# Interleaving layer 0's mixing of one pair with layer 1 of another, and subtracting tanh results before they are weighed

## The chip, the cores and the metric

The kernel runs on one core of a Trainium2 chip. The metric is device time in microseconds (us) of one execution; the numbers below are medians of the runs of a kernel, and lower is better. Every comparison uses runs on the same chip, in rounds in which the kernel before and the other kernel take turns.

The engines are named as the profile names them: PE is TensorE's matmul, PEld its weight loads, DVE is VectorE, ACT ScalarE, POOL GpSimd, SP SyncE. L156 is line 156 of the kernel in question.

## The reference, cut to what matters

Four graph layers run one after another on `x` (8 batches, 2048 nodes, 64 features), each followed by a residual addition and a layer norm over the features. The change concerns the end of layer 0 and all of layer 1:

```python
# layer 0, its end ("mixing")
def attn_scores(f):
    return jnp.tanh(f @ fcW + fcb) @ av
pair = jnp.stack([industry, g], axis=2)
coefs2 = jax.nn.softmax(attn_scores(pair), axis=-1)
out = jnp.einsum('bnk,bnkf->bnf', coefs2, pair)
x = _layernorm(x + out)
# layer 1
A_td = A + jnp.eye(n); dinv = rsqrt(A_td.sum(1)); A_hat = dinv[:, None] * A_td * dinv[None, :]
x = _layernorm(x + jnp.einsum('bnd,kd->bnk', jnp.einsum('bmd,nm->bnd', x, A_hat), W))
# layers 2 and 3: not touched
```

A softmax over two scores is a sigmoid of their difference. So the weights need only `(tanh(f0) - tanh(f1)) @ av`, and whether the subtraction happens before or after the product with `av` is free to choose. A batch pair of layer 1 needs all of that pair's layer 0, but nothing of another pair's.

## The kernel before

The eight batches are four *pairs*; two batches' 64 features sit side by side in 128 columns. The 2048 nodes are four *chunks* of 512. So mixing is 16 chunks, one after another, and then layer 1 takes the four pairs.

```python
def layernorm(pool, r, dst, groups=2 * JT):          # r: 128 x 512, 8 groups of 64
    mean = ...; nc.vector.tensor_reduce(mean, r, AX.X, ALU.add)
    xc = pool.tile([P, groups, F], F32, tag="ln_c", name="ln_c", bufs=1)
    nc.vector.scalar_tensor_tensor(xc, mean..., -1.0 / F, r, op0=ALU.mult, op1=ALU.add)
    nc.scalar.activation(r, xc, AF.Square)
    var = ...;  nc.vector.tensor_reduce(var, r, AX.X, ALU.add)
    vare = ...; nc.vector.tensor_scalar(vare, var, 1.0 / F, EPS, op0=ALU.mult, op1=ALU.add)
    rstd = ...; nc.gpsimd.tensor_tensor(rstd, vare, neg_half[:, :groups], ALU.pow)   # L155
    nc.vector.tensor_tensor(dst, xc, rstd..., ALU.mult)                              # L156

def mm(*args, **kw):                                 # pinned: keeps its place in the stream
    tc.keep_in_program_order(nc.tensor.matmul(*args, **kw))
# ... cut ...
for p in range(NP):                                  # mixing
    for c in range(NCH):
        # four indirect gathers (GpSimd) -> gn;  ut <- u0_hbm
        pg = to_rows(...)                            # four transposes
        nc.scalar.activation(gt, pg, AF.Identity, bias=-1.0)
        nc.tensor.matmul(pi, lhsT=bd_ind, rhs=ut, start=True, stop=True)
        nc.vector.tensor_copy(ind, pi)               # the "ind copy"
        tt = []
        for b in range(2):
            for k, src in enumerate((ind, gt)):
                nc.tensor.matmul(pf, lhsT=fcz[:, b, :], rhs=src, start=True, stop=True)
                nc.scalar.activation(t1, pf, AF.Tanh, bias=fcb_col)
                tt.append((b, k, t1))
        for i, (b, k, t1) in enumerate(tt):          # four weighing products
            nc.tensor.matmul(pd, lhsT=avz[:, b, k, :], rhs=t1, start=i == 0, stop=i == 3)
        nc.scalar.activation(th, pd, AF.Tanh, scale=0.5)
        # three DVE instructions: ind <- gt + (th + 1)/2 * (ind - gt)
        pt = to_rows(...)                            # back: four transposes
        nc.vector.tensor_tensor(r, pt..., r, ALU.add)   # r was loaded with x
        layernorm(mp, grouped(r), grouped(xn[...]))
for p in range(NP):                                  # layer 1
    nc.vector.tensor_tensor(y, xn[:, p], dinv..., ALU.mult)
    u = product(..., plus_identity=True)             # split y in halves, 128 + 32 matmuls
    for c in range(NCH):
        evacuate(ut, u[c]); po = ...                 # four output products
        nc.vector.tensor_tensor(r, po, dinv..., ALU.mult)
        nc.gpsimd.tensor_tensor(r, r, xs, ALU.add)
        layernorm(lp, grouped(r), grouped(xs))
```

An instruction that is pinned with `keep_in_program_order` keeps its place among the pinned instructions of its engine. All others are placed by the scheduler when the kernel is built. Either way an engine's order is then fixed: it does not change at run time. Note that `layernorm` goes from DVE to ACT, back to DVE, to GpSimd for the power, and back to DVE.

Of the kernel before, what the change touches and what calls it, by code (L numbers as in the profile page):

```python
# [30 lines left out]
F32 = mybir.dt.float32  # L31
# [25 lines left out]
def tile_gnn_fast(  # L57
# [144 lines left out]
    hs_hbm = dram.tile([N, BF + 8], F32, name="hs_hbm")  # L202
    gs_hbm = dram.tile([N, BF], F32, name="gs_hbm")
# [427 lines left out]

    hy_scope.close()
    const2 = ctx.enter_context(tc.tile_pool(name="const2", bufs=1))
    xn = const2.tile([P, NP, NT, P], F32, name="xn")
    with tc.tile_pool(name="mix", bufs=1) as mp, tc.tile_pool(name="mix_ps", bufs=1, space=PSUM) as mps:
        bd_ind = on_diagonal(mp, w_ind, "bd_ind")
        fcb_col = column(mp, fc_b, "fcb_col", 1)
        av_col = column(mp, av, "av_col", 1)

        fcz = mp.tile([P, 2, P], F32, name="fcz")  # L640
        nc.vector.memset(fcz, 0.0)

        avz = mp.tile([P, 2, 2, P], F32, name="avz")
        nc.vector.memset(avz, 0.0)
        for b in range(2):
            s = slice(b * F, (b + 1) * F)
            nc.sync.dma_start(fcz[s, b, :], fc_w)
            nc.vector.tensor_copy(avz[:, b, 0, s], av_col.to_broadcast([P, F]))
            nc.vector.tensor_scalar(avz[:, b, 1, s], avz[:, b, 0, s], -1.0, None, op0=ALU.mult)
        g_rows = gs_hbm[:].rearrange("n (p f) -> (n p) f", f=P)  # L650
        for p in range(NP):
            for c in range(NCH):
                gn = mp.tile([P, JT, P], F32, tag="gn", name="gn", bufs=2)
                for j in range(JT):
                    nc.gpsimd.indirect_dma_start(  # L655
                        out=gn[:, j, :], out_offset=None, in_=g_rows,
                        in_offset=bass.IndirectOffsetOnAxis(ap=rank4[:, p, c * JT + j:c * JT + j + 1], axis=0),
                    )
                ut = mp.tile([P, C], F32, tag="ut", name="ut", bufs=3)
                nc.sync.dma_start(ut, u0_hbm[p][:, cols(c)])  # L660
                pg = to_rows(mps, "tr", 2, [gn[:, j, :] for j in range(JT)])
                gt = mp.tile([P, C], F32, tag="gt", name="gt", bufs=2)
                nc.scalar.activation(gt, pg, AF.Identity, bias=-1.0)
                pi = mps.tile([P, C], F32, tag="mm", name="pi", bufs=6)
                nc.tensor.matmul(pi, lhsT=bd_ind, rhs=ut, start=True, stop=True)
                ind = mp.tile([P, C], F32, tag="ind", name="ind", bufs=2)
                nc.vector.tensor_copy(ind, pi)

                tt = []
                for b in range(2):  # L670
                    for k, src in enumerate((ind, gt)):
                        pf = mps.tile([P, C], F32, tag="mm", name="pf", bufs=6)
                        nc.tensor.matmul(pf, lhsT=fcz[:, b, :], rhs=src, start=True, stop=True)
                        t1 = mp.tile([P, C], F32, tag="t1", name="t1", bufs=4)
                        nc.scalar.activation(t1, pf, AF.Tanh, bias=fcb_col)
                        tt.append((b, k, t1))
                pd = mps.tile([P, C], F32, tag="mm", name="pd", bufs=6)
                for i, (b, k, t1) in enumerate(tt):
                    nc.tensor.matmul(pd, lhsT=avz[:, b, k, :], rhs=t1, start=i == 0, stop=i == 3)
                th = mp.tile([P, C], F32, tag="th", name="th", bufs=1)  # L680
                nc.scalar.activation(th, pd, AF.Tanh, scale=0.5)
                nc.vector.tensor_tensor(ind, ind, gt, ALU.subtract)
                nc.vector.scalar_tensor_tensor(ind, th, 1.0, ind, op0=ALU.add, op1=ALU.mult)
                nc.vector.scalar_tensor_tensor(ind, ind, 0.5, gt, op0=ALU.mult, op1=ALU.add)
                pt = to_rows(mps, "tr", 2, [ind[:, cols(j, P)] for j in range(JT)])
                r = mp.tile([P, JT, P], F32, tag="r", name="r", bufs=3)
                load_x(r, p, c)
                nc.vector.tensor_tensor(r, pt.rearrange("p (t f) -> p t f", f=P), r, ALU.add)
                layernorm(mp, grouped(r), grouped(xn[:, p, c * JT:(c + 1) * JT, :]))


    with tc.tile_pool(name="l1", bufs=1) as lp, tc.tile_pool(name="l1_ps", bufs=1, space=PSUM) as lps:
        bd_w1 = on_diagonal(lp, w1_t, "bd_w1")
        for p in range(NP):
            y = lp.tile([P, NT, P], F32, tag="y", name=f"y{p}", bufs=2)
            nc.vector.tensor_tensor(
                y, xn[:, p, :, :], dinv[:, :, None].to_broadcast([P, NT, P]), ALU.mult
            )
            u = product(lp, lps, lambda k, y=y: y[:, k * JT:(k + 1) * JT, :], plus_identity=True)
            for c in range(NCH):  # L700
                ut = lp.tile([P, C], F32, tag="ut", name="ut", bufs=3)
                evacuate(ut, u[c])
                po = lps.tile([P, JT, P], F32, tag="mm", name="po", bufs=4)
                for j in range(JT):
                    nc.tensor.matmul(po[:, j, :], lhsT=ut[:, cols(j, P)], rhs=bd_w1, start=True, stop=True)
                r = lp.tile([P, JT, P], F32, tag="r", name="r", bufs=2)
                ts = slice(c * JT, (c + 1) * JT)
                xs = xn[:, p, ts, :]
                nc.vector.tensor_tensor(
                    r, po, dinv[:, ts, None].to_broadcast([P, JT, P]), ALU.mult  # L710
                )
                nc.gpsimd.tensor_tensor(r, r, xs, ALU.add)
                layernorm(lp, grouped(r), grouped(xs))
# [6 lines left out]
    with tc.tile_pool(name="l2c", bufs=1) as cp:  # L720
# [3 lines left out]
        with tc.tile_pool(name="apt", bufs=1) as ap_:  # L724
# [31 lines left out]
            with tc.tile_pool(name="apt1", bufs=1) as a1, tc.tile_pool(  # L756
                name="apt_ps", bufs=1, space=PSUM
            ) as aps:
                for c in range(NCH):
                    u = [aps.tile([P, C], F32, tag=f"u{p}", name=f"u{p}") for p in range(NP)]  # L760
                    acc = a1.tile([P, C], F32, tag="acc", name="acc", bufs=2)
                    for t in range(NT):
# [9 lines left out]
                        for p in range(NP):  # L772
                            nc.tensor.matmul(  # L773
                                u[p], lhsT=xn[:, p, t, :], rhs=pt, start=t == 0, stop=t == NT - 1
                            )
# [12 lines left out]
        with tc.tile_pool(name="l2", bufs=1) as lp, tc.tile_pool(name="l2_ps", bufs=1, space=PSUM) as lps:  # L788
# [7 lines left out]
            for p in range(NP):  # L796
                u1n = lp.tile([P, NT, P], F32, tag="u1n", name=f"u1n{p}")
                u = product(lp, lps, lambda k, p=p: xn[:, p, k * JT:(k + 1) * JT, :])
# [47 lines left out]
    with tc.tile_pool(name="l3", bufs=1) as lp, tc.tile_pool(name="l3_ps", bufs=1, space=PSUM) as lps:  # L846
# [21 lines left out]
        nc.tensor.matmul(pm, lhsT=bd_v, rhs=b2c, start=True, stop=True)  # L868
        nc.vector.tensor_tensor(b1s, pm, b1, ALU.add)

        pending = []

        def later(n, f):

            pending.append([n, f])

        def tick():
            for e in pending:
                e[0] -= 1
            while pending and pending[0][0] <= 0:  # L880
                pending.pop(0)[1]()

# [829 lines left out]
```

## Time and profile before

2304.5 us, median of four runs (2302.7 to 2307.0). The profiled execution took 2301.2 us.

The lines of its profile are in the prediction: what the engines do in five windows of this kernel. Read them for the stage in which PE stands idle although another stage has plenty of independent PE work. Layers 2 and 3, from 742.6 us to the end, took 1558.6 us; the change doesn't concern them. In a line of the waits the order is: engine, what waits, `<-` the engine and tile that released it, the total in us, how often, the longest. A line of the timeline is start, duration, engine, line, operation, and in brackets how long the engine had been idle and what ended that.

### The profile page before, as it was taken

How to read it: one execution, taken by the hardware profiler on the slowest of the kernel's cores; microseconds unless marked ns; L12 is line 12 of the kernel's file. 1: busy time of each engine (PE TensorE's matmuls, PEld its weight loads, DVE VectorE, ACT ScalarE, POOL GpSimd, SP SyncE). 2: the span in 40 equal slices, each digit the busy share in tenths (PEclk: the TensorE clock that was granted, in tenths of full speed). 3: DMA queues.
4: the chain of work that ended last, by engine and by line, in shares of the span. 5: the costliest groups of instructions: out<-in, count | busy, mean ns of one | idle time of the engine just before them, and what ended most of it. 6: DMA issues, size and time to landing. Idle time of an engine off the chain costs nothing.

```text
span 2301.2 us, 19853 instructions
## 1 busy us (share of the span) xinstructions
PE 2009.9 (87%) x7382; PEld 1293.3 (56%) x7382; DVE 1119.7 (49%) x1895; ACT 361.7 (16%) x610; POOL 468.2 (20%) x432
## 2 busy tenths in 40 slices
PE   5379977887993999979999999999996999899994
PEld 3258863335882444447447446546543777777873
DVE  4347983554544122222882784685585334341322
ACT  2412323331111111101001001000000011111110
POOL 0155524550332332310010010011001001020202
PEclk8779998999995999989999999999998999999997
DMA  7712223220000000010000000000000223210000
GB/s 245 233 38 63 84 95 91 69 60 1 1 1 12 0 19 19 19 41 1 9 8 3 7 7 5 5 10 5 5 7 11 73 70 82 72 30 1 19 1 20
DMA packets 92586, 88.64 MB, mean 39 GB/s; under 512 B 62976, under 2 KB 63232, under 8 KB 92416
## 3 DMA queue, kind: packets, MB, share of 16 engines
q1 hardware_dynamic: 65072, 61.35, 9.3%
q10 hardware_dynamic: 23568, 16.95, 2.5%
q0 software_dynamic: 3840, 8.98, 1.5%
q8 instruction: 60, 0.98, 0.2%
q14 instruction: 46, 0.38, 0.1%
HBM read 66.22 MB, written 21.04 MB: 38 GB/s over the span
## 4 chain that ended last, share of the span: by engine, by line
PE 47%; DMA 8%; DVE 7%; POOL 3%; issue 2%; ACT 1%; SPq 0%; DVEq 0%; ACTq 0%; POOLq 0%
PE py L826 17%; PE u L773 10%; PE u L459 9%; PE u L171 8%; DMA a<-in_adj_t 7%; DVE a L932 2%; POOL ln_r L155 1%; PE pr L171 1%; PE tr L137 1%; DVE xg L115 1%; POOL r L838 1%; DVE ln_c L145 1%; DVE ln_v L151 1%; ACT r L149 0%; PE s L764 0%
## 5 line engine op out<-in xcount | busy, mean ns | idle before, releaser
L826 PE MATMUL py<-wp,xg 128*128 128x512 f32 x1024 | 448.6, 597 | 8.4 <-DVE pr L831 5.7
L826 PEld LDWEIGHTS py<-wp,xg 128*128 128x128 f32 x1024 | 193.6, 191 | 254.4 <-issue 216.3
L459 PE MATMUL u<-adj,vh 128*128 128x512 f32 x768 | 236.2, 410 | 24.7 <-ACT vh L166 20.9
L171 PE MATMUL u<-adj,hi 128*128 128x512 f32 x768 | 255.2, 413 | 0.0
L171 PE MATMUL u<-adj,lo 128*128 128x512 f32 x768 | 246.1, 400 | 1.0 <-DVE lo L897 1.0
L773 PE MATMUL u<-pt,xn 128*128 128x512 f32 x512 | 228.3, 604 | 8.3 <-DVE u L782 7.1
L459 PE MATMUL u<-adj,vl 128*128 128x512 f32 x768 | 228.9, 402 | 0.0
L831 DVE TENSOR_TENSOR pr<-py,emb_n 128x512 f32<-128x512 f32 x256 | 177.0, 691 | 51.9 <-PE py L826 37.4
L832 DVE TENSOR_REDUCE r<-pr 128x32 f32<-128x512 f32 x256 | 175.5, 685 | 8.1
L459 PEld LDWEIGHTS u<-adj,vh 128*128 128x128 f32 x768 | 141.8, 190 | 64.2 <-ACT vh L166 22.7
L773 PEld LDWEIGHTS u<-pt,xn 128*128 128x128 f32 x512 | 97.6, 193 | 130.6 <-issue 116.1
L171 PEld LDWEIGHTS u<-adj,hi 128*128 128x128 f32 x768 | 142.8, 190 | 41.0 <-issue 11.8
L171 PEld LDWEIGHTS u<-adj,lo 128*128 128x128 f32 x768 | 144.1, 189 | 34.5 <-DVE lo L897 1.4
L459 PEld LDWEIGHTS u<-adj,vl 128*128 128x128 f32 x768 | 141.4, 190 | 31.4 <-issue 0.7
L834 POOL TENSOR_TENSOR r<-r,bias 128x256 f32<-128x256 f32 x32 | 23.4, 730 | 636.4 <-DVE r L832 636.4
L155 POOL TENSOR_TENSOR ln_r<-ln_e,neg_half 128x8 f32<-128x8 f32 x64 | 105.7, 1651 | 185.5 <-DVE ln_e L153 185.2
L767 DVE TENSOR_SCALAR pt<-pt 128x512 f32<-128x512 f32 x64 | 48.8, 780 | 173.6 <-ACT pt L766 172.1
L771 POOL TENSOR_TENSOR acc<-acc,pt 128x512 f32<-128x512 f32 x60 | 79.6, 1327 | 163.3 <-DVE pt L767 160.5
L916 POOL TENSOR_TENSOR r<-r,xn 128x512 f32<-128x512 f32 x16 | 20.5, 1278 | 420.9 <-DVE r L915 420.9
L932 DVE SCALAR_TENSOR_TENSOR a<-a,adj 128x512 f32<-128x512 f32 x64 | 44.6, 697 | 124.7 <-DMA a<-in_adj_t 124.4
L156 DVE TENSOR_TENSOR xn<-ln_c,ln_r 128x512 f32<-128x512 f32 x48 | 41.8, 871 | 92.2 <-POOL ln_r L155 92.2
L655 POOL DMA_INDIRECT gn<-gs_hbm,rank x64 | 67.8, 1060 | 81.1 <-PE tr L137 62.3
(292 smaller groups left out, 2418.7 us busy)
## 6 DMA issues: line engine op xcount, KB each, us to landing
a<-in_adj_t SPq DMA_DIRECT2D x64, 256.0 KB, 2.8
a<-in_adj_t SPq DMA_DIRECT2D x16, 512.0 KB, 6.7
a<-in_adj_t ACTq DMA_DIRECT2D x16, 512.0 KB, 6.8
gs_hbm<-acc SPq DMA_DIRECT2D x16, 256.0 KB, 2.0
u_hbm<-ut SPq DMA_DIRECT2D x16, 256.0 KB, 2.8
ut<-u_hbm SPq DMA_DIRECT2D x16, 256.0 KB, 3.1
u_hbm<-u SPq DMA_DIRECT2D x16, 256.0 KB, 2.3
xg<-u_hbm SPq DMA_DIRECT2D x32, 128.0 KB, 2.7
```

Of the source, the lines that this page charges most:

```text
L155: nc.gpsimd.tensor_tensor(rstd, vare, neg_half[:, :groups], ALU.pow)
L156: nc.vector.tensor_tensor(dst, xc, rstd[:, :, None].to_broadcast([P, groups, F]), ALU.mult)
L171: tc.keep_in_program_order(nc.tensor.matmul(*args, **kw))
L459: nc.tensor.matmul(u[c], lhsT=half[:, j, :], rhs=adj[t][:, cols(c)], start=t == 0 and i == 0, stop=ends and not own,)
L655: nc.gpsimd.indirect_dma_start(out=gn[:, j, :], out_offset=None, in_=g_rows, in_offset=bass.IndirectOffsetOnAxis(ap=rank4[:, p, c * JT + j ...
L767: nc.vector.tensor_scalar(pt, pt, 1.0, None, op0=ALU.max)
L771: nc.gpsimd.tensor_tensor(acc, acc, pt, ALU.add)
L773: nc.tensor.matmul(u[p], lhsT=xn[:, p, t, :], rhs=pt, start=t == 0, stop=t == NT - 1)
L826: nc.tensor.matmul(py.rearrange("p o d -> p (o d)"), lhsT=xg[b][:, q, cols(j, P)], rhs=wp[:, q, cols(k)], start=q == 0, stop=q == 1,)
L831: nc.vector.tensor_tensor(pr, py, e_b, ALU.mult)
L832: nc.vector.tensor_reduce(r[:, j, b, cols(k, OH)], pr, AX.X, ALU.add)
L932: nc.vector.scalar_tensor_tensor(a, a, 1.0, adj[t][:, cols(k)].bitcast(F32), op0=ALU.mult, op1=ALU.not_equal, accum_out=left[:, t, k:k + 1],)
```

## The change

The intent: run layer 1 of pair p-1 as filler between mixing's dependent steps of pair p, so that PE never waits for its own result to return; and halve the weighing by subtracting the two tanh results first, on GpSimd. What layer 1 needs of mixing goes through DRAM. The core of the diff, with the cuts marked:

```diff
+    def mix_parts(i):                    # gathers, pi, ind copy, pg, gt   (as before)
+        ...
+        mm(pi, lhsT=bd_ind, rhs=ut, start=True, stop=True)
+        inds[i] = mp.tile([P, C], F32, tag="ind", name="ind", bufs=2)
+        nc.vector.tensor_copy(inds[i], pi)
+    def mix_scores(i):
+        for b in range(2):
+            t1 = []
+            for src in (inds[i], gts[i]):
+                mm(pf, lhsT=fcz[:, b, :], rhs=src, start=True, stop=True)
+                nc.scalar.activation(t1[-1], pf, AF.Tanh, bias=fcb_col)
+            nc.gpsimd.tensor_tensor(t1[0], t1[0], t1[1], ALU.subtract)
+            tts[i].append(t1[0])
+    def mix_weigh(i):
+        for b in range(2):                                   # two products, were four
+            mm(pd, lhsT=avz[:, b, :], rhs=tts[i][b], start=b == 0, stop=b == 1)
+        ...
+    def mix_end(i):
+        ...
+        layernorm(lp, grouped(r), grouped(r))
+        nc.sync.dma_start(x1_hbm[p][:, wide(c), :], r)
+    def l1_parts(p, c):
+        nc.sync.dma_start(y, x1_hbm[p][:, wide(c), :])
+        nc.vector.tensor_tensor(y, y, dinv..., ALU.mult)
+        part[c] = split(lp, y, f"v{c}", 1, [P, JT, P])
+    def layer1(p): ...                    # a generator: one matmul per `yield`
+    steps = NP * NCH
+    for i in range(steps + 1):
+        k = 10 if i > NCH else 0          # the first pair's mixing has no filler
+        if i < steps: mix_parts(i);      fill(k)
+        if i > 0:     mix_weigh(i - 1);  fill(k)
+        if i < steps: mix_scores(i);     fill(k)
+        if i > 0:     mix_end(i - 1);    fill(k)
+        if i == NCH:
+            for c in range(NCH): l1_parts(0, c)
+    ...                                   # the rest of layer 1
```

(In the kernel each `fill` stands under its `if` on a line of its own.) Mixing is now itself a two-stage pipeline: iteration i scores chunk i and weighs chunk i-1. TensorE's order is pinned throughout this stage; the orders of DVE, ACT and GpSimd are left to the scheduler.

## The prediction

> **What bounds the kernel now.** I read the page first: which engine is busiest, and where along the span it is not.
>
> ```profile
> PE 2009.9 (87%) x7382; PEld 1293.3 (56%) x7382; DVE 1119.7 (49%) x1895; ACT 361.7 (16%) x610; POOL 468.2 (20%) x432
> ...
> PE   5379977887993999979999999999996999899994
> ```
>
> TensorE (PE) is the engine of this kernel, near nine tenths nearly everywhere after the start. A digit is 57.5 us. Digits 7 to 10 (7 8 8 7, 345 to 575 us) and digit 13 (3) are holes. By the lines that run there, layer 0's mixing occupies 343 to 545 us, layer 1's products 545 to 693 us, and 693 to 745 us is layer 1's end plus the setting up of layer 2. I then asked for the busy time of each engine in these stretches, and in two stages of the same kernel whose TensorE stream is already ordered by hand (layer 0's slot stage, and layer 3). Columns: microseconds, then busy time of PE, PEld, DVE, ACT, POOL (instructions), granted clock, DMA share, GB/s.
>
> ```profile
> 343.00:545.00 202.00, 151.12 (x416) 68.53 (x416) 101.25 (x170) 69.92 (x113) 94.51 (x80) 0.94 0.26 63
> 545.00:693.00 148.00, 147.05 (x739) 122.42 (x740) 68.33 (x98) 20.47 (x36) 35.99 (x24) 0.99 0.00 1
> 693.00:745.00 52.00, 12.90 (x69) 11.75 (x68) 25.21 (x34) 8.92 (x13) 14.04 (x10) 0.56 0.10 13
> ...
> 141.00:343.00 202.00, 191.14 (x839) 155.07 (x839) 164.97 (x312) 54.12 (x92) 98.64 (x101) 0.95 0.24 73
> ...
> 1800.00:2260.00 460.00, 444.23 (x2076) 352.33 (x2075) 153.44 (x300) 56.37 (x92) 37.96 (x26) 0.99 0.16 41
> ```
>
> Mixing leaves PE idle for 51 us of 202, layer 1 for 1 us of 148, the end and setup for 39 of 52. The two hand-ordered stages keep PE at 191/202 = 95% (with DVE at 82%) and 444/460 = 97%. The waits between 378 and 518 us (12.5 chunks; total, times, longest) say why mixing is slower:
>
> ```profile
> PE pf L673 <- DVE ind L667: 18.2, 13, 1.4
> ...
> PE pf L673 <- ACT gt L663: 8.9, 13, 0.7
> ```
>
> 27.1 us over 12.5 chunks, 2.2 us in each: PE waits for its own result to come back from DVE and ACT. One chunk on the timeline (start, duration):
>
> ```profile
> 400.17 0.68 DVE L667 COPY ind<-pi 128x512 f32<-128x512 f32 x1
> ...
> 400.91 1.12 PE L673 MATMUL pf<-ind,fcz 128*128 128x512 f32 x2 [1.41 <-DVE ind L667]
> ...
> 406.27 3.60 PE L679 MATMUL pd<-t,avz 128*128 128x512 f32 x8
> 406.27 0.19 PEld L679 LDWEIGHTS pd<-t,avz 128*128 128x128 f32 x1 [0.24 <-issue]
> 406.70 0.19 PEld L679 LDWEIGHTS pd<-t,avz 128*128 128x128 f32 x1 [0.24 <-ACT t L675]
> ...
> 411.38 0.68 DVE L667 COPY ind<-pi 128x512 f32<-128x512 f32 x1
> ```
>
> The period is 411.38 - 400.17 = 11.2 us. A 592 ns matmul record starts every 0.43 us (406.27 to 406.70), so the true price of an fp32 pass is 0.43 us, and each fp32 matmul shows as two. In layer 1 the price is the distance between two like instructions one half-step (four 512-wide, one 128-wide) apart, 1.045 us:
>
> ```profile
> 686.24 0.22 PE L464 MATMUL u<-ident_r,vl 128*128 128x128 f32 x1
> ...
> 687.29 0.23 PE L464 MATMUL u<-ident_r,vh 128*128 128x128 f32 x1
> ```
>
> After the last product come four chunks' layer norms, then layer 2's setup:
>
> ```profile
> 692.65 3.84 PE L705 MATMUL po<-bd_w,ut 128*128 128x128 f32 x32
> ...
> 702.33 1.74 DVE L156 TENSOR_TENSOR xn<-ln_c,ln_r 128x512 f32<-128x512 f32 x1 [1.23 <-POOL ln_r L155]
> ...
> 719.96 0.69 DVE L156 TENSOR_TENSOR xn<-ln_c,ln_r 128x512 f32<-128x512 f32 x1 [1.81 <-POOL ln_r L155]
> ...
> 742.64 2.24 PE L764 MATMUL s<-er,el 128*128 128x512 f32 x4 [9.52 <-DVE er L738]
> ```
>
> So 28 us of end (692.5 to 720.7) and 22 us of setup.
>
> **What the Trainium skill says.** "FP8 and Floating Point Precision", TensorE Precision Notes: true fp32 takes four passes through the array. "TensorE: Matmul & The Clock Gate", Wait — 56ns, not 53.3ns?: back to back, a warm 512-wide pass costs 215.7 ns. Four make 0.86 us; the trace has 2 x 0.43, agreed. Layer 1's reduced-precision halves cost (1.045 - 0.12)/4 = 0.23 us, 7% above that figure; I use the trace. The same page, Part 1: an idle window of about 3.4 us halves the clock; 693 to 745 us was granted 0.56, so holes cost twice. "SBUF — State Buffer", Who interferes with whom: a DVE instruction with two SBUF inputs and a GpSimd instruction that reads SBUF exclude each other. The trace agrees: L156 takes 0.69 us alone and 1.74 us at 702.33, where GpSimd's addition began at 702.26.
>
> **The change part by part.**
> *Tanh results subtracted first.* Per chunk `pd` shrinks from 4 to 2 fp32 matmuls: 4 passes x 0.43 = 1.7 us of PE, 16 x 1.7 = 27.5 us. Added: two GpSimd subtractions of 128x512, about 1.3 us each (the accumulation at L771 has a mean of 1327 ns), 2.6 us per chunk. On the path of `pd` it puts 1.3 us in place of nothing, but `pd` now comes one iteration later, so it should hide.
> *PE per mixing chunk after:* 14 passes (pi 2, pf 8, pd 4) x 0.43 = 6.0, plus 8 transposes x 0.12 = 1.0: 7.0 us (before 18 x 0.43 + 1.0 = 8.7).
> *Layer 1 as filler.* A pair is 160 filler units = 32 half-steps, 33.4 us; 40 units go into an iteration, 8.4 us. Output products: 8 passes x 0.12 = 0.96 us a chunk, ten of them in the filled loop, 0.85 us an iteration. Filled iteration: 7.0 + 8.4 + 0.85 = 16.2 us of PE. At the 95% of the slot stage, 17.0 us.
> *Others in a filled iteration.* DVE: 16 instructions of 0.69, a half copy 0.35 and two small 0.17: 11.7 us, some 13 with collisions. GpSimd: four gathers 4 x (1.09 + 0.3 issue) = 5.5, subtractions 2.6, two powers 3.3, one addition 1.3: 12.7 us. ACT about 6. All under 17, so PE should stay the bound.
> *Moved to DRAM.* 20 stores and 32 loads of 256 KB (and one load of 1 MB), 2.0 to 3.1 us each by the page's DMA table, in a stretch whose DMA share was 0.26 and then 0.00: hidden, as they are read at least an iteration later.
> *Sum from 343 us.* Start to the first `pf` is unchanged (355.4). Five iterations are not filled; nothing covers their latencies: 10 us each (GpSimd alone 5.5 + 2.6 + 1.65 = 9.8; PE 7.0), with the cold start and the last one's end until 403. Eleven filled x 17.0 = 187: 590. The last, with half the filling: 4 passes 1.7, transposes 0.5, 20 units 4.2, po 1: 598. Remaining 180 units: 36 x 1.045 = 37.6, four output products 3.8, 3% of waits: 641. End: only two chunks remain instead of four, and before the last two took 6 and 5 us: 16 instead of 28: 657. Setup unchanged, 22: layer 2 starts at 679 instead of 742.6. Gain 63 us; later stages don't change (the four tiles in place of one carry the same instructions).
>
> **The rivals.**
> *The layer norm becomes the bound.* Mixing and layer 1 now share one `ln_c` buffer. At its shortest it is held 4.9 us (the spacing of the last two norms, 715.08 to 719.96), but 6.9 us where gathers stood before the power on GpSimd (403.95 to 410.86). Two norms at 9 to 10 us, with the longer queues, would make 19 to 20 us an iteration: +30 us, 2275. Against: `ln_c` itself isn't on PE's path, the queues only delay.
> *GpSimd queue.* If gathers stand ahead of subtractions, `pd` stalls PE: 14 us in the unfilled iterations, 18.5 in the filled ones: +37 us, 2280. For it: 75% busy, and the port collisions. Against: between the scores and the weighing lie about 8 us of other PE work when filled.
> *Better than the sum.* 16.4 us filled and 8.5 unfilled, as layer 3's 97% suggests: -14 us, 2228.
> *Something hidden anyway.* If layer 2's setup waits for more than the end of layer 1 (buffers of the wider stack), the gain shrinks by 5 to 10 us.
>
> **Range and chances.** The sum gives 2305.3 - 63 = 2242. The first two rivals pull one way more than the third the other, so I take 2247. Range 2228 to 2278. The 2% line is at 2259; the gain has to fall from 63 to under 46 us to miss it, which either of the first two rivals does alone: 0.74 faster, 0.24 same. Slower would need the stream to stall for over 100 us: 0.02.
>
> **What would show it.** Right: PE at 93% or more between the end of the unfilled iterations and the end of layer 1; `pd` with 64 records; filled iterations 16.5 to 17.5 us apart; first layer 2 product near 680 us. Wrong: PE waiting for `ind`, `th` or the GpSimd subtraction inside the filled part (second rival), waits of DVE or PE for `ln_r` and iterations of 19 us or more (first), unfilled iterations far over 10 us, or more than 25 us between layer 1's last norm and layer 2. A change of over 10 us in layers 2 or 3 would say that I overlooked a dependency there.

## The result

After: 2278.3 us, median of four runs (2276.5 to 2279.5), against 2304.5 us. The ratio is 0.9885, with a 95% interval of 0.9868 to 0.9902: within 2%, that is "same" in the terms of the prediction. A ratio is the mean time of one kernel's fast runs over that of the other's of the same rounds, so it isn't quite the ratio of the medians quoted beside it. The prediction had said 2247 with a range up to 2278; the kernel gained 26 us of the 58 forecast.

The page of the kernel after, engine totals and the tenths of PE:

```profile
PE 1989.5 (87%) x7318; PEld 1287.7 (57%) x7318; DVE 1137.8 (50%) x1905; ACT 361.4 (16%) x610; POOL 514.0 (23%) x464
...
PE   5379986988785999979999999999986989999994
```

PE lost 64 instructions (7382 to 7318) and 20 us. POOL gained 32 instructions, the subtractions, and 46 us. The holes of the kernel before are still there in part: digits 7 to 12 are 6 9 8 8 7 8 where full slices would show 9, and digit 13 is a 5. A slice is now 56.9 us.

The windows show where. These are the unfilled iterations, the filled ones, the rest of layer 1, the end and the setup (columns as in the prediction):

```profile
343.00:399.00 56.00, 39.36 (x100) 17.05 (x101) 27.88 (x40) 20.34 (x33) 43.16 (x39) 0.86 0.37 96
399.00:615.00 216.00, 187.95 (x766) 125.75 (x764) 136.45 (x197) 62.64 (x105) 119.98 (x90) 0.96 0.29 77
615.00:682.00 67.00, 52.87 (x245) 42.97 (x246) 31.21 (x51) 8.08 (x14) 18.15 (x13) 0.87 0.23 71
682.00:696.50 14.50, 1.46 (x14) 1.27 (x12) 7.14 (x12) 1.26 (x2) 5.90 (x5) 0.67 0.00 0
696.50:718.60 22.10, 7.08 (x33) 6.95 (x33) 8.03 (x7) 4.77 (x4) 1.67 (x1) 0.50 0.22 30
```

In the filled part PE is at 188/216 = 87%, not 93%. DVE is at 136/216 = 63% and POOL at 56%: no other engine is full either. Eleven iterations took 216 us, 19.6 us each. They aren't alike: the starts of `pi` lie 15.8 to 24.9 us apart, in a pattern that repeats with the four chunks of a pair.

What PE and what DVE waited for in that part (first fence PE, second DVE):

```profile
PE pf L171 <- DVE ind L695: 13.0, 4, 4.8
PE pg L174 <- ACT t L711: 3.9, 4, 1.1
PE pt L174 <- DVE ind L725: 3.9, 3, 2.4
```

```profile
DVE r L156 <- POOL ln_r L155: 29.5, 12, 4.3
...
DVE xn L156 <- POOL ln_r L155: 13.4, 8, 1.8
```

PE's largest wait is once more for the `ind` copy, as before the change; it is 13.0 of the 28 us that PE lost, and the rest is spread over other steps of DVE and ACT. Filling was to have covered it: between `pi` and the first `pf` now lie twenty filler matmuls. But DVE, which makes that copy, waits for 43 us (29.5 + 13.4) for the norm's power on GpSimd. One stall on the timeline shows how the two are joined:

```profile
490.48 1.02 PE L171 MATMUL pi<-ut,bd_ind 128*128 128x512 f32 x2
...
496.65 0.69 DVE L156 TENSOR_TENSOR xn<-ln_c,ln_r 128x512 f32<-128x512 f32 x1 [1.78 <-POOL ln_r L155]
...
501.98 0.69 DVE L156 TENSOR_TENSOR xn<-ln_c,ln_r 128x512 f32<-128x512 f32 x1 [1.81 <-POOL ln_r L155]
...
503.32 0.68 DVE L695 COPY ind<-pi 128x512 f32<-128x512 f32 x1
...
504.05 2.08 PE L171 MATMUL pf<-ind,fcz 128*128 128x512 f32 x2 [4.83 <-DVE ind L695]
```

`pi` is finished at 490.48 + 1.02 = 491.50. The copy of it starts at 503.32, 11.8 us later, although it is ready all that time. Two norms stand in front of it in DVE's order, each with a last step (L156) at which DVE stands still until GpSimd has made the power. These two stops are 3.6 of the 11.8 us (1.78 + 1.81); most of the rest is the norms' own work, which the order has put ahead of the copy. PE then waits for 4.83 us, and the next product runs at half speed (2.08 us in place of 1.02); the clock granted from 504.0 to 506.2 us is 0.50. The Trainium skill, "Perfetto Trace Analysis", Tensor Engine Instruction (MATMUL, LD_WEIGHTS), says that ACT, DVE and GpSimd work strictly first in, first out; the trace agrees, with these 11.8 us.

The end of layer 1 and the start of layer 2:

```profile
681.41 2.05 PE L171 MATMUL po<-bd_w,ut 128*128 128x128 f32 x16 [0.44 <-ACT ut L788]
...
695.52 0.69 DVE L156 TENSOR_TENSOR xn<-ln_c,ln_r 128x512 f32<-128x512 f32 x1 [1.81 <-POOL ln_r L155]
...
718.58 0.77 PE L882 MATMUL s<-er,el 128*128 128x512 f32 x1 [9.52 <-DVE er L856]
```

Layer 2's first product comes at 718.6 us; before it was 742.6. From there to the end the two kernels take the same time, 2276.4 - 718.6 = 1557.8 us and 2301.2 - 742.6 = 1558.6 us. So the change is decided before layer 2.

### The profile page after: what moved, and what is told of

The parts are those of the page before. It is cut to its first block, busy times and chain, and to the rows that moved or that the text cites. A ratio compares the mean times of both kernels' runs of the same rounds, so it can differ in the third digit from the quotient of the medians.

```text
span 2276.4 us, 19888 instructions
## 1 busy us (share of the span) xinstructions
PE 1989.5 (87%) x7318; PEld 1287.7 (57%) x7318; DVE 1137.8 (50%) x1905; ACT 361.4 (16%) x610; POOL 514.0 (23%) x464
## 4 chain that ended last, share of the span: by engine, by line
PE 61%; DMA 12%; DVE 11%; POOL 7%; issue 4%; ACT 2%; SPq 1%; ACTq 0%; DVEq 0%; POOLq 0%
PE py L944 17%; PE u L171 16%; PE u L891 10%; PE u L461 9%; DMA a<-in_adj_t 8%; POOL ln_r L155 3%; DVE a L1038 2%; PE pz L171 2%; PE pf L171 1%; DVE ln_c L145 1%; DVE ln_v L151 1%; PE pr L171 1%; DVE ln_m L143 1%; POOL gn L686 1%; ACT r L149 1%
## 5 line engine op out<-in xcount | busy, mean ns | idle before, releaser
L461 PE MATMUL u<-adj,vh 128*128 128x512 f32 x512 | 158.6, 409 | 15.0 <-ACT vh L166 11.2
L171 PEld LDWEIGHTS u<-adj,hi 128*128 128x128 f32 x768 | 143.2, 190 | 40.8 <-issue 11.2
L461 PE MATMUL u<-adj,vl 128*128 128x512 f32 x512 | 152.1, 398 | 0.0
L461 PEld LDWEIGHTS u<-adj,vh 128*128 128x128 f32 x512 | 96.4, 190 | 45.3 <-ACT vh L166 12.7
L461 PEld LDWEIGHTS u<-adj,vl 128*128 128x128 f32 x512 | 96.5, 189 | 22.1 <-issue 0.7
L149 ACT ACTIVATE r<-ln_c 128x512 f32<-128x512 f32 x64 | 40.4, 631 | 290.6 <-DVE ln_c L145 277.2
```

Of the source, the lines that this page charges most:

```text
L461: nc.tensor.matmul(u[c], lhsT=half[:, j, :], rhs=adj[t][:, cols(c)], start=t == 0 and i == 0, stop=ends and not own,)
```

## The experiments

**Theories.** T (order): the scheduler's fixed DVE order puts ready copies behind norm steps that wait for GpSimd's power; a filled iteration pays 3 us on average. Rival A (buffer): the one `ln_c` buffer that mixing's and layer 1's norms share makes them wait for each other. Rival B (GpSimd's queue): the new subtractions lengthen it, and everything that needs GpSimd comes late. The common measure is the period of an iteration in the filled part: the mean of nine, from the 7th start of a `pi` product to the 16th. In the kernel after it is 179.0/9 = 19.9 us. In the texts on record theory A is this rival A, and theories C and D are T as it stood then: C named the copy alone, D all of DVE's order. Rival E is the way of the norm's result through DRAM, rival F the hand order of TensorE itself. Runs of different rounds are compared through the kernel before, whose medians lie between 2304.3 and 2306.3 us.

### e1: the norm's buffer held for less

The centred values stay in `r`; the shared buffer takes only the squares, from ACT to the reduction.

```diff
-        xc = pool.tile([P, groups, F], F32, tag="ln_c", name="ln_c", bufs=1)
-        nc.vector.scalar_tensor_tensor(xc, mean..., -1.0 / F, r, ...)
-        nc.scalar.activation(r, xc, AF.Square)
+        nc.vector.scalar_tensor_tensor(r, mean..., -1.0 / F, r, ...)
+        sq = pool.tile([P, groups, F], F32, tag="ln_c", name="ln_s", bufs=1)
+        nc.scalar.activation(sq, r, AF.Square)
```

> The changed kernel, in which the layer norms of the merged stage centre in place, so that the one shared buffer is held from the square to the reduction (some 1.5 us) and not until the last multiplication (6.2 us on average). Theory A, the shared ln_c buffer serialises the two norms of an iteration and so fills the DVE queue with waits: the filled iteration falls from 19.8 to 17.5 us or less, the time from 2278 to about 2253 us. Rival B, the GpSimd queue (gathers, subtractions, powers) is what delays: no more than 5 us gained. Rival C, only the place of the copy of ind in the DVE queue counts: 5 to 10 us, as the scheduler draws another order.

Measured: 2275.3 us against 2306.3, ratio 0.9868 [0.9845, 0.989]; period 19.5 us. The buffer is worth at most a few tenths of a microsecond per iteration, so rival A falls.

### e2: the ind copy on another engine

```diff
-        nc.vector.tensor_copy(inds[i], pi)
+        nc.scalar.copy(inds[i], pi)
```

> The changed kernel with the one copy that TensorE waits for most (ind out of PSUM) on ACT instead of DVE. Theory C, that copy stands in DVE's fixed order behind norm steps that wait for GpSimd: the 13 us of waits of pf for ind between 399 and 615 us, and the half-clock passes behind the two of over 4 us, go; 12 to 20 us gained (2260 to 2266). Theory A: the wait only moves to the next consumer of DVE, under 6 us gained. Rival B: nothing gained.

Measured: 2296.7 us against 2306.3, ratio 0.9952 [0.9936, 0.9969]; period 20.4 us. This took 18 us longer than the changed kernel itself. PE's two largest waits in the filled part:

```profile
PE pf L171 <- ACT ind L695: 11.6, 4, 3.6
PE pf L171 <- DVE r L753: 11.6, 4, 4.1
```

The copy is late on ACT too: the first line is the old wait with another engine's name. ACT's order is fixed as well, and its largest wait is for DVE's centring in the norms, which it squares: 48.8 us between 400 and 620. The second line is DVE late in emptying a layer-1 output product, whose PSUM buffer `pf` takes next. I had expected a gain of 12 to 20 us, and by the marks set down this result is rival B's ("nothing gained"); what speaks against B are e3 and e8. As I read the miss, it says that taking one instruction out of the blocked queue does not help as long as the queue it goes to waits on the blocked one.

### e3: four weighing products again, no subtraction on GpSimd

The second tanh is taken of the negated argument, so that the four products add up without a subtraction.

```diff
+    nc.vector.tensor_scalar(fcn_col, fcb_col, -1.0, None, op0=ALU.mult)
-                nc.scalar.activation(t1[-1], pf, AF.Tanh, bias=fcb_col)
-            nc.gpsimd.tensor_tensor(t1[0], t1[0], t1[1], ALU.subtract)
-            tts[i].append(t1[0])
+                if k == 0: nc.scalar.activation(t1[-1], pf, AF.Tanh, bias=fcb_col)
+                else:      nc.scalar.activation(t1[-1], pf, AF.Tanh, bias=fcn_col, scale=-1.0)
+            tts[i] += t1
-        for b in range(2): mm(pd, lhsT=avz[:, b, :], rhs=tts[i][b], start=b == 0, stop=b == 1)
+        for n in range(4): mm(pd, lhsT=avz[:, n // 2, :], rhs=tts[i][n], start=n == 0, stop=n == 3)
```

> The changed kernel without its second part: four tanh tiles are weighed by TensorE again (the second one of each pair taken with the sign turned), nothing is subtracted on GpSimd. TensorE gets 1.7 us more in each of 16 chunks, GpSimd 2.6 us less. Rival B (GpSimd queue): time equal or lower than 2278, as 2.6 us of 12.7 leave the queue. Theories A and C: between 5 and 25 us slower, as TensorE has more to do and waits as before.

Measured: 2294.6 us against 2306.3, ratio 0.9942 [0.9925, 0.9958]; period 20.9 us. Less work on GpSimd and more on PE made it 16 us slower than the changed kernel, so rival B falls: the subtractions are not what holds it up. It also splits the change: the interleaving alone gains 12 us, and the subtraction 13 (by the ratios) to 16 us (by the medians) more on top of it. PE's largest wait between 400 and 640 us was now this:

```profile
PE pf L171 <- DVE r L757: 17.9, 5, 4.7
```

The `ind` copy came only 1.7 us late on average, but DVE was late in emptying layer 1's output products, and DVE still waited 54.5 us there for powers (41.1 and 13.4). Another order, another ready step behind the same stops.

### e4: the subtraction alone, in the kernel before

```diff
-                        tt.append((b, k, t1))
+                        tt.append(t1)
+                    nc.gpsimd.tensor_tensor(tt[2 * b], tt[2 * b], tt[2 * b + 1], ALU.subtract)
-                for i, (b, k, t1) in enumerate(tt):
-                    nc.tensor.matmul(pd, lhsT=avz[:, b, k, :], rhs=t1, start=i == 0, stop=i == 3)
+                for b in range(2):
+                    nc.tensor.matmul(pd, lhsT=avz[:, b, :], rhs=tt[2 * b], start=b == 0, stop=b == 1)
```

> The kernel before with only the second part of the change: tanh results subtracted on GpSimd, two weighing matmuls instead of four, no merging. If mixing was bound by TensorE work: 16 x 1.7 = 27 us gained. If by the chain of waits, as the 2.2 us of waits in each chunk say: the subtraction of 1.3 us puts back most of it, 0 to 10 us gained.

Measured: 2358.4 us against 2306.3, ratio 1.021 [1.0181, 1.0239]: 52 us slower, where I had expected a small gain. Mixing's period went from 11.2 to 15.1 us. PE's wait between 378 and 518 us says why:

```profile
PE pd L679 <- POOL t L676: 30.2, 9, 3.4
```

Without the pipeline that weighs a chunk one iteration later, `pd` needs the subtraction at once, and in GpSimd's order the subtraction stands behind the next chunk's four gathers. So the 27.5 us of PE work (an estimate of the prediction) that the subtraction saves are only had together with the interleaved pipeline, while the interleaving gains 12 us without the subtraction (e3).

### e5: the norm's power left out (a wrong result)

```diff
-        rstd = ...; nc.gpsimd.tensor_tensor(rstd, vare, neg_half[:, :groups], ALU.pow)
-        nc.vector.tensor_tensor(dst, xc, rstd..., ALU.mult)
+        nc.vector.tensor_tensor(dst, xc, vare..., ALU.mult)
```

> Wrong on purpose: in the merged stage the variance itself multiplies in place of its power -1/2, so a norm has no step on GpSimd and DVE has no wait for one; all else is as in the changed kernel. Theory D, the bound of the filled part is DVE's fixed order, 63% busy and 33% standing in waits, of which 43 us of 216 are for the power: the waits of DVE fall by some 40 us, the filled iteration from 19.8 to 17.5 us or less, the time to about 2250 us. Rival E, the DMA round trip of the norm's result through DRAM (16 us of waits of DVE, stores in the way of loads on one queue) is the bound: no more than 8 us gained. Rival F, TensorE's waits come from the tight hand order itself (one chunk ahead): no more than 5 us gained.

Measured: 2228.4 us against 2304.7, ratio 0.967 [0.9654, 0.9686], which is 50 us below the changed kernel; the outputs are wrong, as intended (relative error 0.13). The nine iterations of the kernel after, then those of e5:

```profile
417.90:596.90 179.00, 153.70 (x623) 101.84 (x622) 112.41 (x163) 50.59 (x84) 99.66 (x75) 0.96 0.28 74
```

```profile
404.00:559.30 155.30, 148.36 (x624) 101.26 (x624) 112.46 (x163) 50.70 (x85) 70.08 (x58) 0.99 0.32 85
```

DVE does the same 163 instructions in the same 112 us in both, and yet the period is 155.3/9 = 17.3 in place of 19.9 us, with PE at 96% and the clock at 0.99. So it isn't DVE's amount of work that costs the time; what changed is that DVE no longer stands still for GpSimd. This is close to the predicted 17.0 us for the filled iteration, with one wait out of the way that the prediction didn't have. Rivals E and F, which allowed 8 and 5 us, fall. The scheduler was free to draw another order here, but drew nearly the same: of the 162 DVE instructions that start in those iterations, 148 stand in the order of the kernel after. e5 alone can't say whether the wait matters or the 30 us less of GpSimd work, since it takes both away.

### e6: DVE's order by hand everywhere

All DVE instructions of the merged stage are pinned. The norm is cut in three pieces, and the later pieces are put behind 8 and then 12 further filler matmuls; e1's in-place centring is kept. Not shown in the cut: the power's result has a third buffer, the inputs of the first pair's layer 1 are made one by one in the unfilled iterations, and the reload of one pair from DRAM after the loop comes 60 filler matmuls later (`fill(100)` for `fill(40)`). e8 to e10 keep the third buffer and `fill(100)`. The core:

```diff
+    def norm(r, dst, done=None):
+        ...                                           # mean, centring, square
+        def second():
+            ...                                       # variance, power on GpSimd
+            def third():
+                dv(nc.vector.tensor_tensor(dst, r, rstd..., ALU.mult))
+            later(12, third)
+        later(8, second)
-        nc.vector.tensor_copy(inds[i], pi)
+        dv(nc.vector.tensor_copy(inds[i], pi))        # dv() pins
```

> The changed kernel with DVE's order in the merged stage fixed by hand as TensorE's is: each norm is cut at its two waits (for ACT's square, for GpSimd's power) and the rest comes 8 and 12 filler matmuls later, the scaling of y comes 24 after its load, and the copy of ind keeps its place just behind its product. No instruction is removed. Theory D: DVE's waits in the filled part fall from 70 to under 30 us, the filled iteration to 17 to 17.8 us, the time to 2245 to 2258 us. Rival F: TensorE waits as before, within 5 us of 2278. Rival E: the waits for y stay, 10 us gained at most.

Measured: 2258.6 us against 2304.7, ratio 0.9802 [0.9785, 0.9818]. The filled period fell to 17.5 us, and the mean delay of the `ind` copy (from the end of its product to its start, last ten chunks) from 5.1 to 0.6 us. The expectation that DVE's waits fall under 30 us was wrong: between 402 and 600 us they add up to 62.5 us, and this is the largest of them:

```profile
DVE r L674 <- POOL ln_r L671: 33.9, 10, 3.9
```

In the nine iterations it is 26.3 us, against 35.8 in the kernel after. So most of DVE's standing for the power is still there, and PE has no wait for the copy any more, because the copy no longer stands behind it. But three of the five unfilled iterations rose to 15.2 us (they were 7.9, 12.7 and 13.0): there the pieces were spaced by filler that isn't there.

### e7: the power on DVE, the scheduler's order kept

The power is made by a guess from the bits and two Newton steps, eight more small DVE instructions per norm; GpSimd is out of the norm and nothing is pinned.

```diff
-        nc.gpsimd.tensor_tensor(rstd, vare, neg_half[:, :groups], ALU.pow)
+        nc.vector.tensor_scalar(n0.bitcast(I32), v.bitcast(I32), 1, -1,
+                                op0=ALU.logical_shift_right, op1=ALU.bitwise_xor)
+        nc.vector.tensor_scalar(n1.bitcast(I32), n0.bitcast(I32), 0x5F3759E0, None, op0=ALU.add)
+        for last in (False, True):
+            nc.vector.tensor_tensor(n0, n1, n1, ALU.mult)
+            nc.vector.scalar_tensor_tensor(n0, n0, -0.5, v, op0=ALU.mult, op1=ALU.mult)
+            nc.vector.scalar_tensor_tensor(rstd if last else n1, n0, 1.5, n1, op0=ALU.add, op1=ALU.mult)
```

> The changed kernel with the power -1/2 of the merged stage's norms computed on DVE (a first guess from the bits and two Newton steps, eight more instructions of 128x8) instead of on GpSimd; the scheduler orders DVE. Correct results again. Theory D with the GpSimd power as its main wait: DVE gets some 1.3 us of work for each norm and loses 2.1 us of waiting, and the queue of gathers no longer stands in the path; filled iteration 17 to 18 us, time 2235 to 2252 us. If instead the work of GpSimd as such was the bound, the same. If what counted in the run without the power was the work saved on DVE's path and not the wait: about 2260 to 2275 us, as DVE now has 2.6 us more in an iteration.

Measured: 2260.1 us against 2304.3, ratio 0.9805 [0.9772, 0.9837], with a correct result. The filled period was 19.3 us and the `ind` copy was as late as ever, 5.05 us on average: DVE no longer waited for a power, but it still stood 19.4 us (between 400 and 600 us) at another step of its order, the scaling of `y`, until `y` had come back from DRAM, and PE still waited 10.1 us for the copy. (In e5 DVE stood 18.9 us at that same step and PE lost only 1.3 us to the copy; what a stop costs depends on what stands behind it.) Of the 24 us by which layer 2 starts earlier than in the kernel after, 9 were gained before these nine iterations, 6 in them and 9 behind them. So e7 beats the changed kernel, but not by mending the filled iteration. Its forecast for theory D (17 to 18 us, 2235 to 2252) failed, and the time lies at the edge of what the rival in it named (2260 to 2275: work saved on DVE counts, and not the wait). e9 decides that: with the same work on DVE in another order the period falls.

### e8: DVE's order by hand, in the filled part alone

As e6, but the scheduler keeps the unfilled part, and the norm's last step stands 24 filler matmuls behind the power.

```diff
+    def dv(ins):
+        if state["filled"]:
+            tc.keep_in_program_order(ins)
-            later(12, third)
+            later(24, third)
```

(The minus line is e6's.)

> DVE ordered by hand in the filled part only (before it the scheduler orders, as in the changed kernel), and the last step of a norm put 24 filler matmuls (5 us) behind the power instead of 12. The power stays on GpSimd, with all its work. Theory D: DVE's waits for the power fall from 34 us in the first hand order to under 12, the unfilled iterations come back from 15 to 8 to 13 us, the time to 2240 to 2250 us. If GpSimd's work is the bound and not the place of the wait: no better than 2255.

Measured: 2259.8 us against 2304.3, ratio 0.9798 [0.9762, 0.9833]. The nine iterations:

```profile
428.50:578.90 150.40, 146.97 (x624) 100.94 (x623) 109.87 (x159) 49.47 (x84) 98.78 (x75) 0.99 0.30 86
```

By the total alone this would be the rival's result ("no better than 2255"); the window says otherwise, and it is the decisive line. Against the kernel after (the window above), DVE works 110 us and GpSimd 99 us, as before, with the power still on GpSimd; yet the nine iterations take 150.4 in place of 179.0 us, 16.7 each, with PE at 98%. What was moved is the place of the instructions (with e1's centring in place, which alone was worth 0.4 us, and a third buffer for the power's result; the orders of ACT and GpSimd, which the scheduler fits to it, change too). DVE's wait for the power, 35.8 us in the nine iterations of the kernel after (22.4 + 13.4), is down to this:

```profile
DVE r L679 <- POOL ln_r L676: 1.1, 3, 0.4
```

The total gained less than that, because the switch from one order to the other stumbled: one iteration took 28.7 us, with one wait of 11.9, and after the loop stood waits of 3.2 and 5.6 us.

### e9: e8 with the power on DVE

```diff
-            nc.gpsimd.tensor_tensor(rstd, vare, neg_half[:, :2 * JT], ALU.pow)
+            ...                                       # e7's Newton steps, pinned
-            later(24, third)
+            later(2, third)
```

> Both: DVE by hand in the filled part, and the power on DVE. Theory D: the waits of DVE that are left are those for TensorE itself; filled iteration 16.5 to 17.3 us, time 2228 to 2242 us, the fastest of the correct kernels. If DVE's work becomes the bound: no better than the better one of the two alone.

Measured: 2266.7 us against 2304.3, ratio 0.9835 [0.98, 0.9869]; period 17.5 us, one iteration of 27.9 us at the switch and a wait of 8.0 us at 613. The forecast (16.5 to 17.3 us, 2228 to 2242, "the fastest of the correct kernels") failed; what came is its other branch, no better than the better one of the two alone. Once the order is right, having the power on DVE brings nothing more. Beside e7 the run has a second use: neither has a power on GpSimd, DVE is busy 135.8 us in e7's nine iterations and 133.4 us in these, and yet the period is 17.5 in place of 19.3 us. There too the order makes the difference (and e1's centring in place, which e7 lacks).

### e10: e8 with its stumbles mended

The first pair's last chunk enters layer 1 only 12 filler matmuls after the switch; the last chunk of mixing gets more filler, and (cut here) the last norm and the last pair's last chunk get shorter spacings.

```diff
-            for c in range(NCH):
+            for c in range(NCH - 1):
                 l1_parts(0, c)
+            later(12, lambda: l1_parts(0, NCH - 1, 24))
-            fill(k)                                   # after mix_weigh
+            fill(k if i < steps else 18)
```

> The second hand order (e8) with its two stumbles mended: the last input of pair 0 is scaled after the first filled iteration's own steps and not before them (a wait of 11.9 us), and the last chunk's norm is cut at shorter distances with more filler ahead of it (waits of 3.2 and 5.6 us). Power on GpSimd as in the changed kernel. Theory D: all filled iterations at 16 to 17.5 us, 12 to 18 us better than e8: 2242 to 2249 us. If the stumbles were paid elsewhere anyway: no better than 2255.

Measured: 2250.1 us against 2304.3, ratio 0.9766 [0.9744, 0.9787], with a correct result. The nine iterations and what PE still waited most for in them:

```profile
422.80:576.10 153.30, 147.08 (x624) 100.89 (x622) 113.11 (x161) 50.01 (x85) 98.13 (x75) 0.99 0.31 86
```

```profile
PE pf L171 <- DVE ind L735: 5.2, 2, 3.7
```

153.3/9 = 17.0 us, and layer 2 starts at 687.7 us, 31 us earlier than in the changed kernel. It is the best correct kernel and beats both: 54 us below the one before and 28 below the one changed. A gap of 7.7 us at the switch remains.

### e11: the changed kernel once more

The changed kernel, unaltered, in the rounds of e10.

> The changed kernel as it is, beside the mended order on one chip: 2275 to 2281 us, filled iterations at 19.8 us.

Measured: 2277.8 us against 2304.3, ratio 0.9879 [0.986, 0.9897]. The result, and the stalls at the same chunks, repeat; the period of the nine iterations is 20.0 us.

### The runs side by side

| run | us | ratio to before | filled period, us | PE busy there | mean delay of the ind copy, us |
|---|---|---|---|---|---|
| after | 2278.3 | 0.9885 | 19.9 | 86% | 5.1 |
| e1 buffer | 2275.3 | 0.9868 | 19.5 | | 4.3 |
| e2 copy on ACT | 2296.7 | 0.9952 | 20.4 | | (on ACT) |
| e3 no subtraction | 2294.6 | 0.9942 | 20.9 | | 1.7 |
| e4 subtraction alone | 2358.4 | 1.021 | (no filled part) | | |
| e5 no power (wrong result) | 2228.4 | 0.967 | 17.3 | 96% | 3.2 |
| e6 order by hand | 2258.6 | 0.9802 | 17.5 | 94% | 0.6 |
| e7 power on DVE | 2260.1 | 0.9805 | 19.3 | 90% | 5.05 |
| e8 order by hand, filled part | 2259.8 | 0.9798 | 16.7 | 98% | 2.45 |
| e9 both | 2266.7 | 0.9835 | 17.5 | 94% | 2.3 |
| e10 e8 mended | 2250.1 | 0.9766 | 17.0 | 96% | 2.7 |
| e11 after, again | 2277.8 | 0.9879 | 20.0 | 85% | 5.05 |

Periods and delays are worked out from starts and ends in the traces.

## Why the prediction was wrong

The prediction's own marks, in us from the start, against the trace of the kernel after:

| step | predicted | measured | miss |
|---|---|---|---|
| five unfilled iterations end at | 403 | 399 | -4 |
| eleven filled iterations | 11 x 17.0 = 187 | 216 | +29 |
| last iteration and rest of layer 1 | 51 | 66 | +15 |
| layer 1's end | 16 | 15 | -1 |
| layer 2's setup | 22 | 22 | 0 |
| layer 2 starts at | 679 | 718.6 | +39 |
| layers 2 and 3 | unchanged | 1557.8 (1558.6 before) | -1 |

**The step that failed** is the filled iteration: PE's 16.2 us were taken "at the 95% of the slot stage", and of the other engines it says "All under 17, so PE should stay the bound". It added up busy time per engine. These sums were right: PE's 16.2 us is 16.3 in e8 (146.97/9), DVE's 11.7 to 13 us was 136/11 = 12.4, and GpSimd's 12.7, of which 1.2 is issue that the profile doesn't count as busy, was 120/11 = 10.9. But an engine that works in a fixed order is not a pool of free time. The two norms of a filled iteration each take DVE to GpSimd and back; the scheduler placed the last step of a norm so close behind its power that DVE stood still there, and put ready work (the `ind` copy, on which PE's next product depends) behind it. A queue that is 63% busy held PE to 87%.

That the order is the cause, and not merely present, rests on these results together: with all the work kept and only its place changed, the period is 17.5, 16.7 and 17.0 us (e6, e8, e10), in e6 although DVE still waits 33.9 us for the power; with the same work on DVE and no power on GpSimd, it is 19.3 us in the scheduler's order (e7) and 17.5 us in the hand order (e9). The wait for the power is the largest of the stops, and without it the scheduler's order gives 17.3 us (e5); but when the power is made on DVE (e7), a stop at another step, the load of `y`, stands in front of the copy and PE still waits 10.1 us for it. So the step that failed is the overlap, the claim that work which fits by its sum also fits in its order, and not the power as such.

The prediction also called the way through DRAM "hidden, as they are read at least an iteration later". DVE stood 16.1 us for the loads of `y` in the filled part.

In the expectation of e5 I argued with DVE's busy share and its waiting share adding up to 96%. That sum proves nothing: nearly all idle time of an engine that works in order is put down to some wait. What counts is what stood in front of a piece of work that was ready.

**The 95% was the wrong neighbour.** The slot stage reaches it with DVE at 82%, so a busy DVE isn't itself the trouble. The prediction took this as support. It should have asked where in a filled iteration DVE stops, and what then stands behind.

**The rest of layer 1** was mis-sized by 15 us. Two waits of PE add up to 13 us: 8.1 us for the last mixed chunk (at 628) and 5.0 us for the evacuation of a layer-1 product (at 661). In the trace both stand behind fixed orders too, but not of DVE alone. For the first, the last weighing product is done at 617.9 us, but ACT takes its tanh only at 622.97, behind a norm's square for which ACT waited 4.45 us; then DVE waits 1.81 us for a norm's power and takes the last two steps of the mixing from 626.41. For the second, ACT's queue holds the reload of one pair from DRAM (issued at 660.17, when the store of its last chunk has landed) in front of the evacuation, which runs at 660.62. I ran no kernel that undoes these waits alone, so their share of the 15 us is read and not shown. The clock granted there was 0.87.

**What was right**: the price of the end (15) and of the setup (22), `pd` with 64 records, and the later stages unchanged. The unfilled iterations came out at 9.8 us on average where 10 were predicted, but that is partly luck: they took 7.6, 7.7, 7.9, 12.7 and 13.0 us. The prediction's reason, GpSimd alone needing 9.8 us, doesn't fit the short ones; in e5, without the power, all five took 7.4 to 8.8 us. One reading of the prediction was off without consequence: the 128-wide matmul of a half-step takes 0.06 and not 0.12 us, so the 512-wide ones are nearer 0.24 than 0.23; its sum used the whole half-step.

**The rivals.** The first named 19 to 20 us an iteration and 2275 us, which is nearly what came. Its mechanism, the shared buffer, falls by e1: held for less, 19.5 us. Its other half sentence, "with the longer queues", was closer, and the sign that the prediction gave for it did come: DVE waited 42.9 us for `ln_r`, at 19.6 us an iteration. The prediction set this rival aside with "the queues only delay"; that delay is what PE paid for. The second, GpSimd's queue, named 14 us for the unfilled iterations (measured 9.8) and falls by e3. It is, though, just what happens when the subtraction is made without the pipeline (e4, 52 us slower). The range reached to 2278 because of these rivals; the chance of "same" should have been more than the 0.24 given, as each of the two alone was enough for it.

**Still open.** Layer 2's softmax stage, up to the first products of what follows it, took 344 to 345 us before, after and in e10, but 348 to 349.5 us in e5, e6, e8 and e9, which makes those totals 4 to 5 us worse than their first stages alone would. PE waits for the same things equally long there (after against e8); what differs is the clock. Apart from the stage's two ends, the trace's clock records show 0.5 once for 3.4 us in the kernel after, and three times, 13.6 us in all, in e8. By estimate, 10.2 us more at half speed cost some 5 us. Why the throttle falls more often there is not shown. How much of e5's gain is the wait and how much the 30 us less of GpSimd work is not separated by e5 itself; e6 and e8 show that the order alone suffices for the filled period.

## What to carry to other kernels

When two stages are merged to fill the idle time of one engine, every other engine's fixed order is merged too: for each engine in the loop, write down its order and ask at which instruction it stands still, and what ready work then stands behind. Cut chains that leave an engine and come back (here DVE, GpSimd, DVE) into pieces, and place each later piece as far behind as the other engine's answer takes; if only the bottleneck's order is pinned, that part is left to a scheduler. The first thing to move is the ready work, ahead of the stop (e6); moving the stop itself comes second (e8). Test the two halves of a change apart: here the subtraction alone cost 52 us, and only with the pipeline did it pay.

## What the Trainium skill lacked or had wrong

- "Perfetto Trace Analysis", Identifying the Most-Contended Engine, takes the occupancy of VectorE, ScalarE and GpSimd as the way to the bottleneck and as a fair measure of how near they are to their limit. Here VectorE at 63% (136 of 216 us) set the pace of the filled part through its order: with the same work in another order, 19.9 us an iteration became 16.7 (e8). The same page remarks, under Optimizing Scalar/DVE Operations, that unsaturated engines can cause bubbles on others, and advises to break up instructions; that an in-order engine which waits inside its queue can bind far below full occupancy, and that the place of its instructions then decides, it doesn't say.
- "GPSIMD Engine Reference" has no price for the power that a layer norm needs. The profile of the kernel after shows it, 64 times 1.66 us on a 128x8 tile, with nearly all of GpSimd's idle time before it ended by DVE's input:

```profile
L155 POOL TENSOR_TENSOR ln_r<-ln_e,neg_half 128x8 f32<-128x8 f32 x64 | 106.2, 1659 | 176.4 <-DVE ln_e L153 175.9
```

  In the kernel before, the same operation on 128x16 (at 174.19 us) took 3.32 us, so, as an estimate from these two sizes, it costs about 0.21 us per element of a partition.
- "TensorE: Matmul & The Clock Gate", Back-to-back issue gap, gives about 131 ns as the sustained spacing of 512-wide matmuls that each have a weight load. The reduced-precision fp32 halves of this kernel's layer 1 run as such a stream, and start 237 ns apart (median between 600 and 690 us of the kernel before, where the granted clock is 1.00). The page doesn't say for which type its 131 ns hold. The formula for a single matmul in the same section, 216 ns, is the nearer one.
